# Strip sums of a layer norm: from one TensorE matmul to sixteen small VectorE moves

## The chip, the cores and the metric

The kernel runs on one core of a Trainium2 chip. A core has five engines that run their own instruction queues side by side: TensorE (PE in the profile; its weight loads are listed as PEld), VectorE (DVE), ScalarE (ACT), GpSimd (POOL) and SyncE (SP), which here issues the DMA transfers. They wait for each other by semaphores. The metric is the device time of one execution in microseconds (us). Three runs of the kernel before took 3235.81, 3236.75 and 3239.74 us: median 3236.75 us.

## The reference, cut to what matters

64 graphs of 256 nodes with 512 features each go through three attention steps. `x` is (64, 256, 512), `adj` is (64, 256, 256), all in fp32.

```
# layer 0, 8 heads of 64
Q, K, V = x @ W_q + b_q, x @ W_k + b_k, x @ W_v + b_v
scores  = Q K^T / 8 + (x @ w_g[:D])[:, :, None] + (x @ w_g[D:])[:, None, :] + b_g + log(adj + 1e-9)
y       = softmax(scores) V + x
# layer 1, first half: 8 heads, second half: 1 head of 512
def attention(h, heads, W, a_src, a_dst):
    n = (h - mean(h)) * rsqrt(var(h) + 1e-6) * g + b          # over the 512 features
    v = n @ W;  s = v . a_src;  t = v . a_dst                 # per head
    e = leaky_relu(s[i] + t[j], 0.2) + adj[i, j]
    return softmax(e over j) v + h
z   = attention(y, 8, W1, ...)
out = attention(z, 1, W2, ...)
```

What the change touches is `rsqrt(var(h) + 1e-6)`, the row factor of every node in both norms ("y norm" and "z norm" below), and how the factor of the rows `s` reaches all partitions in the last step.

## The kernel before, in words

**Layout.** Activations are kept transposed: `xT`, `yT` and `zT` are [128 partitions, 4, 256], features across partitions and nodes along the free dimension. The features are permuted so that a block of 32 x 32 stands in each strip of 32 partitions, which is what VectorE's transposition works on.

**The work of one graph** is a generator, `graph(b)` (L477). Every `yield` ends a step; the steps have names in the lists below. In order: `load` (DMA of X and adj), `turn` (X and adj transposed on VectorE, sums for the Winograd products on GpSimd, xT written to DRAM), `V`, `V7`, `V4`, `Q`, `Q7`, `Q4`, `K`, `K7`, `K4` (products of 2 x 2 blocks in seven multiplications instead of eight, `winograd`, L310: five products, then the seventh, then the fourth), two `scores` (matmul and exp), two `mask` (times adj, sum over j), `sums 0` (L378: column sums on TensorE, reciprocal on VectorE, through DRAM to all partitions; x fetched back), `product 0` (L414: attention times V on TensorE), `gather 0` (scaled and added to x on VectorE, which gives yT; begins `rstd_of`), `tokens 1` (ends `rstd_of`), `V1`, `V1 7`, `V1 4` (products with W1, scaled by the row factor as they leave PSUM), `rows 1` (row factors of the 8 heads through DRAM to all partitions), eight steps `weights` (Relu and Exp on ScalarE, adding adj on VectorE), `sums 1`, `product 1`, `gather 1` (gives zT, begins `rstd_of` again and writes Z + bias to DRAM), `tokens 2` (ends `rstd_of`, fetches the rows X2), `V2`, `V2 7`, `V2 4`, `rows 2`, `weights 2`, and two `product 2` (L748 on: TensorE product, reciprocal `rinv`, ScalarE scales, GpSimd adds, SyncE writes the rows out).

**Order.** TensorE's order is written out by hand: `start`, then `period` repeated (an entry is the age of a graph and a step, so six graphs are in flight at once), then `finish`. `tc.manual_schedule` holds TensorE to it. The other engines get their order from the framework's scheduler, which places what is ready as it goes; their queues are then fixed too and run strictly in order. PSUM is a ring of eight banks (`ps`, L159), given out in TensorE's order; a bank is free when its reader is done. The small scaled copies that wait for a partner product (`m1`, `m5`, `u2`) share a ring of four buffers (tag `kept`).

**The norm statistics** (`rstd_of`, L255). `Z` is the strip-wise transposition of yT or zT: [128, 8, 128], where partition 32a + r of block `b` holds a quarter `a` of the features of node 32b + r. `bn_stats` on each of the 8 blocks (L263) gives count, mean and squared deviations of even and odd elements: 6 numbers, so `parts` is [128, 8, 2, 3]. The four quarters of one node lie in four strips of 32 partitions. To add them, before squares the means into the count's place (L265), multiplies by `same` on TensorE (L268; four copies of the 32 x 32 identity in every strip: every partition gets the sum over the four strips), picks its own blocks with `own` (L273), adds up (L278), and forms the variance as mean of squares less square of mean in L282 to L290. `skew` (L289) keeps the worst ratio of squared mean to variance, since this form loses digits where it is large. GpSimd raises to the power -0.5 (L292).

**Row factors** (`target_rows`, L440). For the single head, exp(-0.8 s) of 256 nodes has to stand on all partitions. Usually it goes through DRAM: VectorE transposes (L460), four small transfers write it (L463), one reads it back to all partitions (L473). For the last graph alone (L442) VectorE spreads it to a tile `wide` and TensorE multiplies by the identity (L447 to L450), which leaves the rows in PSUM.

**Guards.** At the end, `note_odd` (L369) tests collected values against bounds, and a slow path recomputes all graphs if any is out of bounds. Collected are `seen` (sums from ScalarE), `extremes` (the running maximum and minimum of all `rinv`, two VectorE operations a graph, L768) and `skew`. `note_odd` of `seen` stands beside the last graph's `rows 2` (L901); that of `extremes` and `skew` is the last work before the final transposition (L906 to L911).

Of the kernel before, what the change touches and what calls it, by code (L numbers as in the profile page):

```python
# [9 lines left out]
F32 = mybir.dt.float32  # L10
# [4 lines left out]
P = 128  # L15
# [5 lines left out]
def kernel(  # L21
# [49 lines left out]
    extremes = const.tile([P, 2, NT], F32, name="extremes")  # L71
    nc.gpsimd.memset(extremes, 1.0)
# [10 lines left out]
    same = const.tile([P, 4, 32], F32, name="same")  # L83
    own = const.tile([P, 4], F32, name="own")
    nc.gpsimd.memset(own, 0.0)
    for a in range(4):
        strip = slice(32 * a, 32 * a + 32)
        nc.gpsimd.tensor_copy(
            same[strip], ident[strip, strip].unsqueeze(1).to_broadcast([32, 4, 32])
        )  # L90
        nc.gpsimd.memset(own[strip, a : a + 1], 0.125)
    skew = const.tile([P, NT], F32, name="skew")
    nc.gpsimd.memset(skew, LOW)

# [57 lines left out]
    with ExitStack() as main:  # L152
# [102 lines left out]
        def rstd_of(xT):  # L255
# [6 lines left out]
            for block in range(2 * KC):  # L262
                nc.vector.bn_stats(parts[:, block].rearrange("p h c -> p (h c)"), Z[:, block, :])  # L263
            mean = parts[:, :, :, 1]
            nc.vector.tensor_tensor(parts[:, :, :, 0], mean, mean, ALU.mult)  # L265
            yield Z
            pt = ps("st")[:, : 12 * KC]
            nc.tensor.matmul(  # L268
                pt, same.rearrange("p c r -> p (c r)"), parts.rearrange("p b h c -> p (b h c)"),
                start=True, stop=True,  # L270
            )
            picked = small.tile([P, NT, 4, 6], F32, name="picked", tag="picked")
            nc.vector.tensor_tensor(  # L273
                picked, pt.rearrange("p (t g i) -> p t g i", t=NT, g=4),
                own.unsqueeze(1).unsqueeze(3).to_broadcast([P, NT, 4, 6]), ALU.mult,
            )
            means = small.tile([P, NT, 3], F32, name="means", tag="means")
            nc.vector.tensor_reduce(  # L278
                means, picked.rearrange("p t g (h c) -> p t c g h", c=3), AX.XY, ALU.add
            )  # L280
            square = small.tile([P, NT], F32, name="square", tag="square")
            nc.vector.tensor_tensor(square, means[:, :, 1], means[:, :, 1], ALU.mult)  # L282
            var = small.tile([P, NT], F32, name="var", tag="var")
            nc.vector.tensor_tensor(var, means[:, :, 0], square, ALU.subtract)
            nc.vector.scalar_tensor_tensor(
                var, means[:, :, 2], 1.0 / 64.0, var, ALU.mult, ALU.add
            )
            nc.vector.scalar_tensor_tensor(square, var, -16.0, square, ALU.mult, ALU.add)
            nc.vector.tensor_tensor(skew, skew, square, ALU.max)  # L289
            nc.vector.tensor_scalar(var, var, 1e-6, None, ALU.add)  # L290
# [78 lines left out]
        def note_odd(v, low, high):  # L369

            bad = work.tile([P, HD + H], F32, name="bad", tag="kept", bufs=4)[:, : v.shape[1]]
            worst = small.tile([P, 1], F32, name="worst", tag="worst")
            for bound, op in ((low, ALU.max), (high, ALU.min)):
                nc.vector.scalar_tensor_tensor(bad, v, bound, v, op, ALU.not_equal)
                nc.vector.tensor_reduce(worst, bad, AX.X, ALU.max)
                nc.vector.tensor_tensor(odd, odd, worst, ALU.max)
# [63 lines left out]
        def target_rows(st, heads, b):  # L440

            if heads == 1 and b == B - 1:  # L442
# [34 lines left out]
        def graph(b):  # L477
# [270 lines left out]
            rinv = small.tile([P, NT], F32, name="rinv2", tag="rinv2")  # L748
            for t in range(NT):
# [16 lines left out]
                if t == NT - 1:  # L766
                    for i, op in enumerate((ALU.max, ALU.min)):
                        nc.vector.tensor_tensor(extremes[:, i], extremes[:, i], rinv, op)  # L768
# [356 lines left out]
```

## Time and profile before

| what | value |
| --- | --- |
| profiled execution, its own time | 3234.22 us |
| its span, first to last instruction | 3232.4 us |
| median of the three runs | 3236.75 us |
| busy: TensorE / VectorE / ScalarE / GpSimd | 97% / 84% / 68% / 33% |
| one graph in the steady part (L268 at 1545.39 and at 1594.12) | 48.7 us |
| TensorE's strip matmul, L268 | 256 instructions, 41.5 us |
| VectorE's L265, the first small operation behind bn_stats | 128 instructions, 154.9 us |

How to read it: times in a timeline are microseconds from the start of the span, first the start, then how long. Small VectorE operations overlap: the next one starts before the former has ended, so the distance from start to start says what one costs in a queue, and the mean duration does not. `out<-in` gives the tiles by name. `[0.54 <-ACT m L525]` is idle time in front of an instruction and what ended it. A TensorE group of the timeline, say `x8`, covers the whole product.

The profiled execution lies 2.5 us (0.1%) under the median of the runs.

### The profile page before, as it was taken

How to read it: one execution, taken by the hardware profiler on the slowest of the kernel's cores; microseconds unless marked ns; L12 is line 12 of the kernel's file. 1: busy time of each engine (PE TensorE's matmuls, PEld its weight loads, DVE VectorE, ACT ScalarE, POOL GpSimd, SP SyncE). 2: the span in 40 equal slices, each digit the busy share in tenths (PEclk: the TensorE clock that was granted, in tenths of full speed). 3: DMA queues.
4: the chain of work that ended last, by engine and by line, in shares of the span. 5: the costliest groups of instructions: out<-in, count | busy, mean ns of one | idle time of the engine just before them, and what ended most of it. 6: DMA issues, size and time to landing. Idle time of an engine off the chain costs nothing. (4 is left out here: it accounts for less than half of the span.)

```text
span 3232.4 us, 77827 instructions
## 1 busy us (share of the span) xinstructions
PE 3135.6 (97%) x28232; PEld 2621.6 (81%) x28232; DVE 2717.1 (84%) x6093; ACT 2188.5 (68%) x5959; POOL 1068.4 (33%) x1315
## 2 busy tenths in 40 slices
PE   7899999999999999999999999999999999999986
PEld 5678888888888888888888888888888888888864
DVE  5788888888888888888888888888888888888885
ACT  3467677677677677676676676676676676676673
POOL 3232332332332332333333333333323423423333
PEclk9999999999999999999999999999999999999998
DMA  4234444444444444444444444444444434444432
GB/s 133 92 118 131 124 131 131 126 127 133 127 128 133 127 124 135 128 122 134 129 122 136 125 126 124 131 130 125 132 124 132 132 123 133 131 123 133 125 116 90
DMA packets 354664, 407.94 MB, mean 126 GB/s; under 512 B 117840, under 2 KB 262496, under 8 KB 354272
## 3 DMA queue, kind: packets, MB, share of 16 engines
q1 hardware_dynamic: 353120, 401.83, 41.6%
q8 instruction: 224, 3.67, 0.5%
q14 instruction: 168, 1.38, 0.1%
q10 hardware_dynamic: 1152, 1.06, 0.1%
HBM read 266.83 MB, written 135.87 MB: 125 GB/s over the span
## 5 line engine op out<-in xcount | busy, mean ns | idle before, releaser
L682 DVE TENSOR_TENSOR ET<-ET,AT 128x512 f32<-128x512 f32 x512 | 363.4, 711 | 239.3 <-ACT ET L676 238.7
L686 ACT ACTIVATE ET<-ET,ends 128x256 f32<-128x256 f32 x1024 | 482.1, 503 | 104.7 <-DVE ET L682 103.6
L676 ACT ACTIVATE ET<-R,f 128x256 f32<-128x256 f32 x1024 | 461.3, 501 | 74.9 <-PE ps_num L425 55.7
L425 PE MATMUL ps_num<-ET,V 128*32 128x256 f32 x8192 | 466.7, 379 | 0.0
L302 POOL TENSOR_TENSOR S<-yT 128x256 f32<-128x256 f32 x64 | 47.7, 746 | 1210.5 <-ACT zT L409 967.6
L765 POOL TENSOR_TENSOR X<-X,weighted 128x256 f32<-128x256 f32 x256 | 210.9, 834 | 545.0 <-ACT weighted L764 536.9
L425 PEld LDWEIGHTS ps_num<-ET,V 128*32 128x32 f32 x8192 | 263.9, 110 | 155.2 <-issue 1.1
L613 DVE TENSOR_TENSOR ET<-ET,AT 128x1024 f32<-128x1024 f32 x256 | 306.6, 1231 | 39.4 <-ACT ET L599 39.4
L599 ACT ACTIVATE ET<-ps_sc,V 128x512 f32<-128x512 f32 x512 | 302.3, 697 | 7.8 <-PE ps_sc L592 7.8
L756 PE MATMUL ps_av<-V,ET 128*128 128x258 f32 (+1 forms) x1024 | 250.7, 389 | 24.3 <-DVE ET L744 24.3
L326 PE MATMUL ps_a<-w,S 128*128 128x264 f32 (+1 forms) x1024 | 268.5, 385 | 4.9 <-ACT m L639 2.9
L326 PE MATMUL ps_b<-w,S 128*128 128x264 f32 (+1 forms) x1024 | 266.6, 383 | 0.8 <-DVE w L131 0.7
L592 PE MATMUL ps_sc<-QT,KT 64*128 64x256 f32 x2048 | 239.4, 383 | 0.0
L263 DVE BATCH_NORM_STATS2 parts<-Z 128x6 f32<-128x128 f32 x1024 | 238.3, 275 | 0.1
L756 PEld LDWEIGHTS ps_av<-V,ET 128*128 128x128 f32 x1024 | 189.8, 196 | 48.9 <-issue 13.0
L326 PEld LDWEIGHTS ps_a<-w,S 128*128 128x128 f32 x1024 | 185.9, 189 | 46.7 <-ACT m L639 6.9
L326 PEld LDWEIGHTS ps_b<-w,S 128*128 128x128 f32 x1024 | 193.8, 189 | 32.5 <-PE ps_a L326 1.1
L592 PEld LDWEIGHTS ps_sc<-QT,KT 64*128 64x128 f32 x2048 | 192.4, 187 | 24.8 <-issue 1.5
L646 ACT ACTIVATE V<-ps_a,rstd 128x257 f32<-128x257 f32 (+1 forms) x128 | 60.0, 469 | 199.2 <-PE ps_a L326 199.2
L434 DVE TENSOR_TENSOR ps_num<-ps_num,R 128x512 f32<-128x512 f32 x256 | 169.9, 687 | 9.6 <-DMA R<-kept 7.0
L702 POOL TENSOR_TENSOR Z<-Z,bw 128x1024 f32<-128x1024 f32 x64 | 175.7, 2745 | 4.1 <-DVE parts L263 3.0
L409 ACT ACTIVATE yT<-yT,columns 128x256 f32<-128x256 f32 x256 | 120.8, 499 | 65.4 <-DMA yT<-kept 65.4
(175 smaller groups left out, 7396.3 us busy)
## 6 DMA issues: line engine op xcount, KB each, us to landing
R<-kept SPq DMA_DIRECT2D x128, 512.0 KB
X<-in_x_dram SPq DMA_DIRECT2D x256, 128.0 KB
kept<-xT SPq DMA_DIRECT2D x64, 512.0 KB
yT<-kept SPq DMA_DIRECT2D x64, 512.0 KB
R<-kept SPq DMA_DIRECT2D x512, 64.0 KB
kept<-yT SPq DMA_DIRECT2D x64, 512.0 KB
kept<-Z SPq DMA_DIRECT2D x64, 512.0 KB
X<-kept SPq DMA_DIRECT2D x512, 64.0 KB
```

Source lines behind the costliest of these rows:

```text
L263: nc.vector.bn_stats(parts[:, block].rearrange("p h c -> p (h c)"), Z[:, block, :])
L326: nc.tensor.matmul(to, A[:, kk, :], B[:, kk, :], start=(first and kk == 0), stop=(kk == 1), skip_group_check=not first,)
L425: nc.tensor.matmul(num[32 * a : 32 * a + 32, m * N : (m + 1) * N], V[:, j, a // 2, a % 2 * P + q * DH + 32 * m :][:, :32], pair[a // 2][:, ...
L592: nc.tensor.matmul(banks[h % 2][:, o : o + N], KT[lo : lo + DH, (q + h) // 2, j * P : (j + 1) * P], QT[lo : lo + DH, (q + h) // 2, :], sta ...
L599: nc.scalar.activation(ET[:, j, i::2, :], banks[i].rearrange("p (h n) -> p h n", n=N), AF.Exp, bias=c[:, j, :],)
L613: nc.vector.tensor_tensor(ET[:, j, :, :], ET[:, j, :, :], AT[:, j, :].unsqueeze(1).to_broadcast([P, 4, N]), ALU.mult,)
L676: nc.scalar.activation(ET[:, j, h, :], R[q][:, h, :], AF.Relu, bias=f[:, j, at : at + 1])
L682: nc.vector.tensor_tensor(two, two, AT[:, j, :].unsqueeze(1).to_broadcast([P, 2, N]), ALU.add)
L686: nc.scalar.activation(ET[:, j, i, :], ET[:, j, i, :], AF.Exp, bias=targets[:, j, 4 * q + i : 4 * q + i + 1],)
L702: nc.gpsimd.tensor_tensor(Z, Z, folded["2"].row.unsqueeze(1).to_broadcast([P, 2 * KC, P]), ALU.add)
L756: nc.tensor.matmul(av[:, :width], ET[:, j, t * P : (t + 1) * P], V2[:, j, n, :width], start=(j == 0), stop=(j == NT - 1),)
L765: nc.gpsimd.tensor_tensor(o[:, cols], o[:, cols], weighted, ALU.add)
```

## The change

Four edits, and new lists.

1. `rstd_of`: the matmul with `same`, the product with `own` and the small operations behind it go. In their place 16 VectorE copies bring, for every pair of strips, the 32 partitions x 2 x 6 numbers of strip `a`'s blocks `g` and `g + 4` to strip `g` of a tile `gathered`, and two `bn_aggr` combine four quarters each to mean and variance. One addition of 1e-6 remains. `same`, `own` and `skew` go.
2. `target_rows`: the way through TensorE is taken for the last three graphs instead of the last one.
3. `rinvs` keeps the inverse sums of all graphs (two columns a graph) in one tile, which replaces `extremes` and its two operations a graph. Those up to graph 55 are tested beside the last graph's `rows 2`, the other 16 columns at the end.
4. `note_odd`: one clamp by both bounds, one comparison, one reduction, one maximum: four operations in a row instead of two chains of three.
5. `start`, `period` and `finish` are new. In a period V1 and its seventh product now come ahead of V, and "V1 4" behind "V7"; `load` moves to the front.

```diff
-            mean = parts[:, :, :, 1]
-            nc.vector.tensor_tensor(parts[:, :, :, 0], mean, mean, ALU.mult)
+            gathered = small.tile([P, NT, 4, 6], F32, name="gathered", tag="gathered")
+            for a in range(4):
+                for g in range(4):
+                    nc.vector.tensor_copy(
+                        gathered[32 * g : 32 * g + 32, :, a, :],
+                        parts[32 * a : 32 * a + 32, g::4].rearrange("p t h c -> p t (h c)"),
+                    )
             yield Z
-            pt = ps("st")[:, : 12 * KC]
-            nc.tensor.matmul(
-                pt, same.rearrange("p c r -> p (c r)"), parts.rearrange("p b h c -> p (b h c)"),
-                start=True, stop=True,
-            )
-            picked = small.tile([P, NT, 4, 6], F32, name="picked", tag="picked")
...
-            nc.vector.tensor_tensor(skew, skew, square, ALU.max)
-            nc.vector.tensor_scalar(var, var, 1e-6, None, ALU.add)
+            moments = small.tile([P, NT, 2], F32, name="moments", tag="moments")
+            for t in range(NT):
+                nc.vector.bn_aggr(moments[:, t, :], gathered[:, t].rearrange("p a c -> p (a c)"))
+            var = small.tile([P, NT], F32, name="var", tag="var")
+            nc.vector.tensor_scalar(var, moments[:, :, 1], 1e-6, None, ALU.add)
...
-            for bound, op in ((low, ALU.max), (high, ALU.min)):
-                nc.vector.scalar_tensor_tensor(bad, v, bound, v, op, ALU.not_equal)
-                nc.vector.tensor_reduce(worst, bad, AX.X, ALU.max)
-                nc.vector.tensor_tensor(odd, odd, worst, ALU.max)
+            nc.vector.tensor_scalar(bad, v, low, high, ALU.max, ALU.min)
+            nc.vector.tensor_tensor(bad, bad, v, ALU.not_equal)
+            nc.vector.tensor_reduce(worst, bad, AX.X, ALU.max)
+            nc.vector.tensor_tensor(odd, odd, worst, ALU.max)
...
-            if heads == 1 and b == B - 1:
+            if heads == 1 and b >= B - 3:
...
-            rinv = small.tile([P, NT], F32, name="rinv2", tag="rinv2")
+            rinv = rinvs[:, NT * b : NT * b + NT]
...
-                if t == NT - 1:
-                    for i, op in enumerate((ALU.max, ALU.min)):
-                        nc.vector.tensor_tensor(extremes[:, i], extremes[:, i], rinv, op)
...
         period = [
-            (3, "V1 4"), (5, "tokens 2"), (2, "scores"), (2, "scores"), (1, "V4"),
-            (3, "rows 1"), (2, "mask"), (5, "V2"), (3, "weights"), (2, "mask"),
-            (5, "V2 7"), (2, "sums 0"), (2, "product 0"), (5, "V2 4"), (1, "Q"),
-            (5, "rows 2"), (1, "Q7"), (4, "sums 1"), (2, "gather 0"), (3, "weights"),
-            (3, "weights"), (3, "weights"), (5, "weights 2"), (4, "product 1"),
-            (0, "turn"), (1, "Q4"), (1, "K"), (1, "K7"), (3, "weights"),
-            (5, "product 2"), (1, "K4"), (5, "product 2"), (3, "weights"),
-            (2, "tokens 1"), (0, "V"), (2, "V1"), (3, "weights"), (4, "gather 1"),
-            (2, "V1 7"), (0, "V7"), (-1, "load"), (3, "weights"),
+            (4, "weights"), (3, "V1 7"), (1, "V"), (1, "V7"), (5, "tokens 2"),
+            (3, "V1 4"), (3, "rows 1"), (2, "scores"), (2, "scores"), (2, "mask"),
+            (-1, "load"), (2, "mask"), (1, "V4"), (3, "weights"), (5, "V2"),
+            (5, "V2 7"), (2, "sums 0"), (2, "product 0"), (5, "V2 4"), (5, "rows 2"),
+            (1, "Q"), (1, "Q7"), (4, "sums 1"), (3, "weights"), (3, "weights"),
+            (2, "gather 0"), (5, "weights 2"), (0, "turn"), (3, "weights"),
+            (3, "weights"), (4, "product 1"), (2, "tokens 1"), (1, "Q4"), (1, "K"),
+            (1, "K7"), (5, "product 2"), (4, "gather 1"), (1, "K4"), (5, "product 2"),
+            (3, "weights"), (3, "weights"), (2, "V1"),
         ]
...
+                    note_odd(rinvs[:, : NT * (B - 8)], 1e-25, 1e25)
                     note_odd(seen[:, : 4 * B], -1.0, 1e25)
                     note_odd(seen[:, 4 * B :], -1.0, 3600.0)
...
-        note_odd(extremes.rearrange("p i t -> p (i t)"), 1e-25, 1e25)
-        note_odd(skew, LOW, 0.0)
+        note_odd(rinvs[:, NT * (B - 8) :], 1e-25, 1e25)
```

## The prediction

> **What bounds the kernel now.** I read the share of busy time first, then busy time by stretch, then TensorE's waits in the steady part, then the rows of the instructions that the change touches, and last one period in order of time.
>
> ```profile
> PE 3135.6 (97%) x28232; PEld 2621.6 (81%) x28232; DVE 2717.1 (84%) x6093; ACT 2188.5 (68%) x5959; POOL 1068.4 (33%) x1315
> ```
> ```profile
> 300.00:2800.00 2500.00, 2484.74 (x22678) 2089.66 (x22680) 2146.21 (x4814) 1750.62 (x4784) 833.65 (x1023) 1.00 0.43 129
> ```
> ```profile
> PE ps_a L333 <- ACT m L525: 14.7, 25, 1.7
> ```
>
> The second line has the columns stretch, length, then busy time of PE, PEld, DVE, ACT and POOL, and the granted clock. From 300 to 2800 us TensorE is busy 99.4% at full clock, and its only listed wait there (to 2900 us) is 14.7 us, on ScalarE's copies in the K product. One graph takes 48.7 us there (the strip sums' matmul of the z norm stands at 1545.39 and again at 1594.12 us), so this wait is 0.28 us a graph. VectorE has 14% idle. So TensorE's work sets the time, as long as the others keep their appointments inside the period; the question is whether they still do.
>
> ```profile
> L268 PE MATMUL ps_st<-parts,same 128*128 128x48 f32 x256 | 41.5, 244 | 6.4 <-DVE parts L265 6.3
> ```
> ```profile
> L265 DVE TENSOR_TENSOR parts<-parts 128x16 f32<-128x16 f32 x128 | 154.9, 1210 | 0.1
> L666 DVE TENSOR_SCALAR f<-ends 128x16 f32<-128x16 f32 x64 | 10.7, 167 | 0.0
> L768 DVE TENSOR_TENSOR extremes<-extremes,rinv 128x2 f32<-128x2 f32 x128 | 41.3, 361 | 0.0
> ```
> ```profile
> 1531.29 1.19 DVE L258 STREAM_TRANSPOSE Z<-yT 128x1024 f32<-128x1024 f32 x1
> 1532.40 0.92 DVE L682 TENSOR_TENSOR ET<-ET,AT 128x512 f32<-128x512 f32 x1
> 1533.24 1.63 DVE L263 BATCH_NORM_STATS2 parts<-Z 128x6 f32<-128x128 f32 x8
> 1534.80 0.67 DVE L682 TENSOR_TENSOR ET<-ET,AT 128x512 f32<-128x512 f32 x1
> 1535.39 0.17 DVE L265 TENSOR_TENSOR parts<-parts 128x16 f32<-128x16 f32 x1
> 1535.58 0.88 DVE L744 SCALAR_TENSOR_TENSOR ET<-R,f,AT 128x256 f32<-128x256 f32 x2
> ```
> ```profile
> 1537.93 0.38 ACT L525 COPY m<-ps_b 128x256 f32<-128x256 f32 x1
> 1538.19 0.52 ACT L686 ACTIVATE ET<-ET,ends 128x256 f32<-128x256 f32 x1
> 1538.61 0.72 ACT L517 ACTIVATE AT<-AT,eps 128x512 f32<-128x512 f32 x1
> 1539.22 0.51 ACT L686 ACTIVATE ET<-ET,ends 128x256 f32<-128x256 f32 x1
> 1539.62 0.36 ACT L525 COPY u<-ps_a 128x256 f32<-128x256 f32 x1
> ```
> ```profile
> 1540.03 1.16 PE L333 MATMUL ps_a<-S,wk 128*128 128x128 f32 x8
> ```
>
> The last three fences are one stretch on three engines. VectorE runs it without a gap; ScalarE's copy u, in order behind exponentials and AT+eps that need VectorE, ends just as TensorE starts the seventh K product, which needs it. That appointment has no slack.
>
> **What goes, per graph (two norms).** On TensorE the strip matmul: its two instructions push the next one back 0.25 us in the y norm (1508.10 to 1508.35) and 0.16 in the z norm (1545.39 to 1545.55): 0.40 us. On VectorE, by the distance from start to start: L265 2.4 us (0.17 in the y norm; 2.38 at 1501.98, where it stands until GpSimd's 2.77 us Z<-Z,bw L702, begun at 1501.55, ends), the small operations L273 to L289 2.2, the two extremes 0.6: 5.2 us.
>
> **What comes, per graph.** 32 copies of 32 partitions x 12 elements, 4 bn_aggr, one of the old small operations kept per norm. No row of before is a VectorE operation that reads one group of 32 partitions and writes another. Bounds: two small operations that don't depend on each other follow at 0.08 us (L458 at 1509.58, L666 at 1509.66); two that do, at 0.20 (L288 at 1510.12, L289 at 1510.32). So 16 cost 1.3 to 3.2 us. I take 0.167, the whole duration of L666, the nearest in size and kind (one input, SBUF to SBUF), without overlap: 2.7 us a norm. I lean away from the 0.08 since each copy changes the output's partitions, which no overlapped pair of before does. bn_aggr has no row; 0.07 to 0.2 by the same rows, 0.3 a pair. Sum per graph 5.4 + 0.6 + 0.2 = 6.2 us against 5.2: VectorE stays at about 88% of a period and doesn't become the bound by its sum.
>
> [...]
>
> **Where it falls.** In the new program the 16 copies stand in one block straight behind the eight bn_stats; the old chain let L682 and others in between. Behind the y block now come the pair L744 and the next L682, and on ScalarE the exponentials of that L682, AT+eps and copy u stand in this order. Replayed with the rows: bn_stats done 1534.85; copies to 1537.55; L744 pair 0.8; L682 0.6, 1538.95; exponential pair 0.85, 1539.8; AT+eps 0.6; u 0.3, 1540.7. K's seventh product starts 1540.75. Without any stall it would start at 1534.70 + 5 x 0.895 = 1539.18: stall 1.57, of which the old lists paid 0.28 on average. The cover is 2.0 us: up to 0.125 a copy, L682 is done before ScalarE asks.
>
> VectorE's queue goes on: AT transposes 0.7, bn_aggr 0.3, L682 0.6, L691 1.1, three KT puts 1.0, L434 and L438 twice each 2.4, rinv 0.1, L682 0.6, xT 1.2: rinv of the second strip at about 1547.1. Then L682 (behind GpSimd, 0.3) 1547.9, Z 1549.05, L682 1550.0, on ScalarE two exponentials and u of V1, 1551.3. TensorE is at V1's seventh product at 1540.75 + 0.9 + 1.75 + 0.9 + 1.75 + 5 x 0.89 = 1550.5: another stall of 0.9. The new lists put V1 ahead of V and "V1 4" behind V7, so xT and the puts of V1 have 1 to 5 us of cover; this hides the z block (copies end 1554.3, the put of c that frees the buffer for V's m5 at 1554.8, product 3 of V due 1555.8).
>
> Waits added and steps moved: bn_aggr waits for the copies, with a put of V (y: L682, L691) queued behind it on VectorE, and GpSimd's rstd behind that; both norms' rstd are due more than 5 us later (V1's first scaled copy after 1546.9, V2 after "V4"), so nothing; if that cover went, 0.6 us a graph. SyncE issues ten transfers less (rows of two graphs). The step "load" moves to the front of the period with its eight issues (X 2.4 us of SP, A 1.8), but X still stands ahead of the fetch of X2 and of kept<-rows, as at 1504.74 to 1511.67, and SP has idle stretches behind (1516.1 to 1520.4): nothing; at most 2.4 us of delay to R, which ScalarE takes up some 3 us after it has landed.
>
> Per graph: +1.57 - 0.28 + 0.9 - 0.40 = +1.8 us. 58 graphs run in the steady part (about 250 to 3100 us): +104 us. The other six save the matmul alone: -2.4.
>
> **Start and end.** Fewer GpSimd constants (4 copies of 0.29 us and some memsets) lie beside the first loads: nothing; if they were not covered, -1.9. The row factor of graphs 61 and 62 on TensorE replaces rows through DRAM: TensorE's waits of 12.6 us (3166 to 3179) and 5.2 us (3197.4 to 3202.6) before ps_av. The first is the time of the last graph's own weights, which stays on the chain; of the second the last graph's rstd comes earlier by at most 3.1 us (3209.9 now; 3206.8 by bn_stats from 3201.1, copies, aggr, pow), -3.1. The end: 3.1 us from the last rinv (3222.14) to the last odd (3225.2) become four dependent operations of 0.2 or so: -2.1. note_odd of the early inverse sums is 4 operations beside the last graph. One-off costs of the new start and finish lists are not readable from rows: -5 to +10, taken as 0.
>
> The sum is made against the profiled execution, 3234.2 us (span 3232.4 and 1.8 around it), 2.5 under the median of the runs, within 0.1%. 3234.2 + 104 - 2.4 - 5.2 = 3330.6: forecast 3330, its own range 3270 to 3380 (each stall off by half).
>
> **Rivals.**
> *The cover holds: faster.* Copies follow at 0.08: the block is 1.3 us, K's seventh product stays where it is, V1's stall shrinks to 0 to 0.15. Then -0.40 or -0.25 a graph: 58 of these, -2.4, -5.2 give 3203 to 3212. For it: VectorE's sum hardly grows, the new lists give V1 slack. It decides below 2.0 us a block (0.125 a copy), where the two stalls together just eat the matmul's 0.40.
>
> *Copies collide with GpSimd.* L702 starts as the last bn_stats of the z norm ends, that is under the copies. If a copy must stand aside as L265 does, the z block ends 2.8 us later, V's m5 buffer comes free at 1557.6, ScalarE copies until 1557.95, product 3 of V is 2.2 us late: +128 us, 3458; with GpSimd waiting instead, the put of V1 waits behind L691 and half of it is lost, 3394. For it: the 2.38 us row. Against it: one-input operations run beside GpSimd freely in before (bn_stats), and only two-input rows are stretched. [...]
>
> *The change does little:* stalls of 0.4 take the 0.4 saved, end gains aside: 3230 to 3240.
>
> **How the numbers follow.** Forecast 0.40, collision 0.28, cover holds 0.28, little 0.04. A change of under 0.2% (6.5 us) can't be told from none. Faster: cover holds, less a bit: 0.27. Same 0.04, slower 0.69. The range must reach the fast case (3203) and into the collision case; 3200 to 3440 leaves out half of the collision's full price and the far ends, about 2 in 10.
>
> **What would show it.** Copy rows by start to start: 0.08, 0.17, or some of 2.8 us under L702's successor. TensorE waits on ScalarE's copies in K (u) and in V1 (u), 1 to 1.6 us each, once per graph; period of the scores 50.5 us against 48.7. L268 gone. ps_av waits at the end shorter. I am wrong if the copies overlap, if ScalarE's order has more slack than this one period shows (it is a period with a stall of 0.54; others have less), or if the start and finish lists cost tens of us.

## The result, and the profile after

The kernel after takes 3689.96 us (median of four runs, 3684.24 to 3692.77) against 3236.49 us: a ratio of 1.140, 95% interval 1.138 to 1.142. The prediction was 3330 us with a range of 3200 to 3440. The profiled execution took 3684.24 us, with a span of 3682.4.

The share of busy time, and the stretch from 300 to 2800 us (columns as in the prediction):

```profile
PE 3265.2 (89%) x27984; PEld 2660.5 (72%) x27984; DVE 3005.0 (82%) x7237; ACT 2205.9 (60%) x5959; POOL 1092.9 (30%) x1304
```
```profile
300.00:2800.00 2500.00, 2256.93 (x19517) 1847.14 (x19516) 2069.40 (x4986) 1533.08 (x4153) 742.87 (x890) 0.96 0.36 112
```

TensorE, busy 99.4% of this stretch before, is busy 90%, at a granted clock of 0.96 instead of 1.00. VectorE is not full either: 83%. A graph takes 55.98 us instead of 48.72 (distance of the bn_stats of the y norm over 46 graphs). The difference of 7.26 us, times the 58 graphs of the steady part, is 421 of the 453 us lost; the rest lies in fill and end.

TensorE's waits between 300 and 3300 us (total, times, longest). In a Winograd product ScalarE makes copies of single products, `m` and `u`; a "put" below is the VectorE operation that adds such a copy to another product and writes a finished block.

```profile
PE ps_b L299 <- ACT m L498: 187.3, 54, 3.5
PE ps_a L306 <- ACT u L498: 79.5, 53, 1.9
PE ps_a L299 <- ACT u L612: 19.1, 52, 0.5
```

The second is the wait in K that the prediction replayed: 1.50 us a graph. The third is V1's: 0.37. The first, the largest, it had not: 3.47 us a graph in V, before the fifth product in the order of issue ("product 3 of V" in the prediction). (L299 and L306 were L326 and L333; L498, L612 and L621 were L525, L639 and L648.) The rows of the moves on the page:

```profile
L254 DVE COPY gathered<-parts 32x12 f32<-32x12 f32 x2048 | 586.9, 287 | 25.6
L261 DVE BATCH_NORM_AGGREGATE moments<-gathered 128x2 f32<-128x24 f32 x256 | 46.2, 221 | 0.0
```

The mean of 287 ns hides two kinds. In the y norm sixteen copies take 2.82 us, in the z norm 6.84. VectorE's y block of one period, then its z block in order of time, the whole block first, then five of its copies one by one, then the put that follows:

```profile
1735.77 2.82 DVE L254 COPY gathered<-parts 32x12 f32<-32x12 f32 x16
...
1752.43 6.84 DVE L254 COPY gathered<-parts 32x12 f32<-32x12 f32 x16
...
1752.77 2.23 DVE L254 COPY gathered<-parts 32x12 f32<-32x12 f32 x1
1755.01 0.66 DVE L254 COPY gathered<-parts 32x12 f32<-32x12 f32 x1
1755.69 0.67 DVE L254 COPY gathered<-parts 32x12 f32<-32x12 f32 x1
1756.37 0.67 DVE L254 COPY gathered<-parts 32x12 f32<-32x12 f32 x1
...
1757.23 0.61 DVE L254 COPY gathered<-parts 32x12 f32<-32x12 f32 x1
...
1759.31 0.49 DVE L621 SCALAR_TENSOR_TENSOR V<-ps_c,rstd,m 128x264 f32<-128x264 f32 x1
```

GpSimd in the same time:

```profile
1752.59 2.38 POOL L675 TENSOR_TENSOR Z<-Z,bw 128x1024 f32<-128x1024 f32 x1 [0.36 <-DVE parts L250]
1754.93 0.72 POOL L275 TENSOR_TENSOR S<-zT 128x256 f32<-128x256 f32 x1
1755.61 0.72 POOL L278 TENSOR_TENSOR S<-zT 128x256 f32<-128x256 f32 x1
1756.30 0.72 POOL L276 TENSOR_TENSOR S<-S,zT 128x256 f32<-128x256 f32 x1
1757.09 0.72 POOL L277 TENSOR_TENSOR S<-zT,S 128x256 f32<-128x256 f32 x1
```

Each of the five long copies ends as one of these five operations ends (1752.77 + 2.23 = 1755.00 beside 1752.59 + 2.38 = 1754.97, and so on), and GpSimd's next operation starts before the copy that follows (1754.93 beside 1755.01, the others 0.07 to 0.14 us ahead). The same holds in all 53 z blocks between 300 and 3300 us: five copies over 0.25 us in each, and each of these 265 ends 0.02 to 0.04 us behind the end of one of the five operations. The eleven others take 0.14 to 0.17 us. Then ScalarE and TensorE:

```profile
1759.89 0.38 ACT L498 COPY m<-ps_b 128x257 f32<-128x257 f32 x1 [5.08 <-DVE V L621]
```
```profile
1755.91 1.03 PE L299 MATMUL ps_a<-wv,S 128*128 128x257 f32 x4
1760.41 1.84 PE L299 MATMUL ps_b<-wv,S 128*128 128x257 f32 x4 [3.47 <-ACT m L498]
1762.05 1.92 PE L299 MATMUL ps_a<-wv,S 128*128 128x257 f32 x4
```

The put of c (L621) stands behind the copies, it frees the buffer for ScalarE's m, and TensorE's next product needs the bank that m reads. Behind the wait two products take 1.84 and 1.92 us instead of 1.03: the granted clock is 0.50 from 1760.63 to 1764.04 (lines in the last section). Of the 50 waits of this kind between 300 and 3100 us, 48 were followed by such a stretch. From the start of the product that waited to the end of the next scores product it took 8.5 us on average over all 50, and 6.5 behind the two that were not: 2.0 us a graph.

Together V's wait 3.47, the clock behind it 2.0, K's wait 1.50 less the 0.28 of before, V1's 0.37, less the 0.40 of the strip matmul make 6.7 of the 7.26 us; what the rest consists of is not shown.

### The profile page after: what moved, and what is told of

Its sections match the earlier page's. It is cut to its first block, busy times and chain, and to the rows that moved or that the text cites. A ratio compares the mean times of both kernels' runs of the same rounds, so it can differ in the third digit from the quotient of the medians.

```text
span 3682.4 us, 78506 instructions
## 1 busy us (share of the span) xinstructions
PE 3265.2 (89%) x27984; PEld 2660.5 (72%) x27984; DVE 3005.0 (82%) x7237; ACT 2205.9 (60%) x5959; POOL 1092.9 (30%) x1304
## 5 line engine op out<-in xcount | busy, mean ns | idle before, releaser
L254 DVE COPY gathered<-parts 32x12 f32<-32x12 f32 x2048 | 586.9, 287 | 25.6
L655 DVE TENSOR_TENSOR ET<-ET,AT 128x512 f32<-128x512 f32 x512 | 388.3, 760 | 238.3 <-ACT ET L649 238.2
L299 PE MATMUL ps_b<-wv,S 128*128 128x257 f32 x512 | 181.9, 490 | 210.7 <-ACT m L498 207.8
L265 POOL TENSOR_TENSOR rstd<-var,mhalf 128x2 f32<-128x2 f32 x128 | 96.4, 753 | 789.2 <-DVE var L263 784.5
L299 PE MATMUL ps_a<-w,S 128*128 128x264 f32 (+1 forms) x1024 | 277.4, 394 | 36.5 <-ACT u L612 21.7
L299 PEld LDWEIGHTS ps_b<-wv,S 128*128 128x128 f32 x512 | 113.8, 234 | 251.4 <-issue 234.2
L738 POOL TENSOR_TENSOR X<-X,weighted 128x256 f32<-128x256 f32 x256 | 233.0, 930 | 146.4 <-ACT weighted L737 146.4
L299 PE MATMUL ps_b<-w,S 128*128 128x264 f32 (+1 forms) x1024 | 269.8, 386 | 0.5 <-ACT m L612 0.5
L299 PEld LDWEIGHTS ps_a<-w,S 128*128 128x128 f32 x1024 | 185.1, 191 | 97.2 <-ACT u L612 56.7
L565 PE MATMUL ps_sc<-QT,KT 64*128 64x256 f32 x2048 | 247.1, 391 | 0.0
L498 ACT COPY m<-ps_b 128x257 f32<-128x257 f32 (+1 forms) x128 | 47.2, 369 | 308.3 <-DVE V L621 299.9
L306 PE MATMUL ps_a<-S,wk 128*128 128x128 f32 x1024 | 144.4, 284 | 95.9 <-ACT u L498 89.0
```

The costliest lines, as they stand in the source:

```text
L254: nc.vector.tensor_copy(gathered[32 * g : 32 * g + 32, :, a, :], parts[32 * a : 32 * a + 32, g::4].rearrange("p t h c -> p t (h c)"),)
L299: nc.tensor.matmul(to, A[:, kk, :], B[:, kk, :], start=(first and kk == 0), stop=(kk == 1), skip_group_check=not first,)
L306: nc.tensor.matmul(to[:, m * P : (m + 1) * P], B[:, kk, m * P : (m + 1) * P], A[:, kk, :], start=(first and m == kk == 0), stop=(kk == 1), ...
L565: nc.tensor.matmul(banks[h % 2][:, o : o + N], KT[lo : lo + DH, (q + h) // 2, j * P : (j + 1) * P], QT[lo : lo + DH, (q + h) // 2, :], sta ...
L655: nc.vector.tensor_tensor(two, two, AT[:, j, :].unsqueeze(1).to_broadcast([P, 2, N]), ALU.add)
L738: nc.gpsimd.tensor_tensor(o[:, cols], o[:, cols], weighted, ALU.add)
```

## The experiments

Theories: **A**, the z block, torn by GpSimd, makes most of the loss; **B**, the new lists do; **C**, the number of moves alone, as forecast. All ratios are to runs of the kernel before on the same chip (medians 3236 to 3241 us); times without an interval are single runs. "us a graph" is the distance of bn_stats over 46 graphs.

| run | us | ratio, 95% interval | us a graph |
| --- | --- | --- | --- |
| after | 3690 | 1.140 (1.138 to 1.142) | 55.98 |
| y_moves_only | 3338 | 1.031 (1.029 to 1.032) | 50.31 |
| z_moves_only | 3530 | 1.089 (1.087 to 1.091) | 53.43 |
| moves_by_reduce | 3438 | 1.062 (1.060 to 1.064) | 52.06 |
| no_z_addition | 3433 | | 51.85 |
| reduce_by_target | 3438 | 1.061 (1.059 to 1.062) | 52.07 |
| copies_by_target | 3691 | | 55.98 |
| moves_in_strip | 3443 | | 52.02 |
| reduce_in_strip | 3318 | 1.025 (1.023 to 1.026) | 50.11 |
| five_kept | 3618 | 1.118 (1.116 to 1.119) | 54.69 |
| lists_on_before | 3439 | 1.061 (1.060 to 1.063) | 51.82 |
| moves_old_lists | 3677 | 1.135 (1.133 to 1.137) | 55.54 |
| reduce_by_target_old_lists | 3470 | 1.070 (1.069 to 1.072) | 52.31 |
| no_moves | 3327 | 1.026 (1.025 to 1.028) | 50.49 |
| no_moves_old_lists | 3231 | 0.998 (0.997 to 0.999) | 48.55 |
| tail_alone | 3245 | 1.001 (1.000 to 1.002) | 48.79 |
| moves_by_dma | 3814 | 1.178 (1.177 to 1.180) | 58.05 |

### Which of the two blocks

`rstd_of` gets a flag: copies in the y norm alone in one kernel, in the z norm alone in the other; the norm without them takes its blocks from `parts`.

```diff
-        def rstd_of(xT):
+        def rstd_of(xT, move):
...
-                nc.vector.bn_aggr(moments[:, t, :], gathered[:, t].rearrange("p a c -> p (a c)"))
+                take = gathered[:, t].rearrange("p a c -> p (a c)") if move else parts[:, 4 * t : 4 * t + 4].rearrange("p b h c -> p (b h c)")
+                nc.vector.bn_aggr(moments[:, t, :], take)
```

> The kernel after with the sixteen copies in the y norm alone; in the z norm bn_aggr reads four blocks of one strip from parts, so the z statistics are those of other numbers. The prediction put the whole loss into this block (stalls of 1.57 in K and 0.9 in V1): by it 3330. Theory A (the torn z block makes 5.3 of the 7.3 us a graph): K's and V1's waits stay as in the kernel after, 1.5 and 0.4 us, V's goes: 50 to 51 us a graph, 3310 to 3370.

> The counterpart: copies in the z norm alone, the y statistics are those of other numbers. By the prediction the z block is hidden: 3205, or 3327 as without any moves. Theory A: torn by GpSimd to 5 to 7 us, V's third product waits 2.5 to 3.5 us for ScalarE's copy m and runs slowly behind it: 53 to 56 us a graph, 3500 to 3680.

TensorE's waits, first with the moves in y alone:

```profile
PE ps_a L308 <- ACT u L500: 86.3, 58, 1.9
PE ps_a L301 <- ACT u L614: 19.4, 53, 0.5
```

With the moves in z alone:

```profile
PE ps_a L301 <- DVE V L623: 149.7, 56, 3.5
PE ps_a L308 <- ACT m L500: 81.2, 56, 2.6
```

With the y block alone the time is 3338 us, near the 3330 that the prediction had for the whole change, with K's wait at 1.49 us (forecast 1.57) and V1's at 0.37 (0.9). The z block, forecast as hidden, makes a wait of 2.7 us a graph, here for VectorE's put of V itself; K's wait is for the copy m here, not for u. A graph takes 55.98 us with both blocks and 50.31 with the y block alone, so the z block costs 5.67 us, which fits the 3.47 of V's wait and the 2.0 of the clock. With both blocks copied the time is 352 us above that of the y block alone. C as the whole story falls.

### What makes the z block long

```diff
-                    nc.vector.tensor_copy(
+                    nc.vector.tensor_reduce(
                         gathered[32 * g : 32 * g + 32, :, a, :],
-                        parts[32 * a : 32 * a + 32, g::4].rearrange("p t h c -> p t (h c)"),
+                        parts[32 * a : 32 * a + 32, g::4].rearrange("p t h c -> p t (h c)").unsqueeze(3),
+                        AX.X, ALU.max,
```

> The kernel after, each of the sixteen copies written as a tensor_reduce with maximum over an axis of one element: the same numbers move between the same strips, by another VectorE operation. If only the copy has to take turns with GpSimd (theory A with a mode that belongs to the copy), no move is stretched beyond 0.3 us, the z block takes as long as the y block (2.8 to 3.5 us), the wait for the scaled copy in V goes, and the time is 3290 to 3400 us. If any small VectorE operation gives way to GpSimd, the z block stays near 6.8 us and the time near 3690. Theory B: 3690. Theory C: 3690 is not explained by it at all, and nothing changes here.

The moves of one stretch (shortest, median and longest in ns) and TensorE's waits:

```profile
L254 DVE TENSOR_REDUCE gathered<-parts x615: 135/157/163, 1000.0 to 1989.8; 32x12 f32<-32x12 f32 x154
```
```profile
PE ps_a L307 <- ACT u L499: 79.4, 57, 1.8
PE ps_a L300 <- ACT m L499: 63.1, 56, 1.2
PE ps_a L300 <- ACT m L613: 51.3, 56, 0.9
```

No move is stretched, though 304 of the 614 that start in this stretch run beside an operation of GpSimd; both blocks take 2.69 us, the clock stays at 1.00 between 300 and 2800 us, and 252 us are gone. So of copy and reduction only the copy is stretched beside GpSimd (up to 2.23 us in the block above; none of these reductions took more than 0.163). The time ends above the 3290 to 3400 expected: three waits of 1.4, 1.1 and 0.9 us remain. ScalarE's work stands in another order here than in the kernel after (in V1 the wait is for m, not for u), so these waits are not those of the kernel after one by one.

```diff
-            nc.gpsimd.tensor_tensor(
-                Z, Z, folded["2"].row.unsqueeze(1).to_broadcast([P, 2 * KC, P]), ALU.add
-            )
```

> The kernel after without GpSimd's addition of the bias to Z, which stands beside the z block's third copy (this addition is left out; the bias is zero in these inputs). Theory A: the copy that took 2.23 us takes 0.17, the four others beside the S operations stay at 0.6 to 0.7 each: z block 4.8 us, V's wait 1.2 to 1.6 instead of 3.5, hardly a slow product behind it: 51.5 to 53 us a graph, 3420 to 3510. If the block's length has another cause, 6.8 and 3690.

```profile
L254 DVE COPY gathered<-parts x624: 144/166/676, 1000.4 to 1988.8; 32x12 f32<-32x12 f32 x156
```
```profile
PE ps_a L306 <- ACT u L498: 89.3, 58, 1.8
PE ps_b L299 <- ACT m L498: 78.2, 56, 1.4
```

The copy of 2.23 us is gone, those of 0.6 to 0.68 stay, the z block is 4.77 us, V's wait 1.40, and no wait is followed by slow products: the clock is 1.00 from 300 to 2800 us. As A expected: one operation of GpSimd, 2.1 us of stretch, is worth some 257 us.

### What one move costs

Three kernels change the strips between which a move goes or their order: `gathered[32 * a ...]` written from `parts[32 * a ...]` (in strip), and the two loops exchanged (by target).

> The kernel after, with every copy writing to the strip that it reads (the same sixteen operations of 32 x 12 numbers, but the four quarters of a node are not brought together, so the statistics are those of other numbers: this part of the computation is changed). Tells what changing strips costs. If a copy is held until the last has ended because its output begins in another strip, the y block of 2.82 us falls to 1.3 to 1.7 us (0.08 to 0.1 a copy, three of four in the same strip as their predecessor). Otherwise it stays at 2.8. The z block: under theory A it still meets GpSimd, 4 to 6 us, with fewer interruptions since it is shorter; time 3450 to 3650. Under theory C it follows the y block, about 3250.

> The kernel after with the moves as tensor_reduce over an axis of one, and the two loops exchanged, so that four moves in a row write the same strip. The result of the computation is that of the kernel after. If a move is held only where the strip it writes changes, 12 of 16 cost 0.075 and 4 cost 0.17: a block is 1.6 us (1.3 to 1.8); if the strip it reads counts too, it stays at 2.7. At 1.6 us the block is inside the cover of 2.0 us that the prediction read for K's seventh product, nothing collides with GpSimd, and by theory C the time is 3200 to 3240; by theory B it stays above 3300.

> The kernel after with the two loops of the copies exchanged: four in a row write the same strip, and read four different ones. Copies inside one strip took 0.075 us, copies that change both strips 0.176; as tensor_reduce, four writes to one strip from four strips took 0.169. If the strip that is written decides, the y block is 1.6 us here (and it was the reduction that is slow by itself); if the strip that is read, or a difference between the two, decides, it stays at 2.8. The z block is torn as in the kernel after, less often if it is shorter; time 3440 to 3450 (short) or 3690 (long).

> The kernel after with the moves as tensor_reduce that write the strip they read (statistics of other numbers: the quarters are not brought together). Not torn by GpSimd, and short if what holds a move is the change of strips: 1.3 to 1.7 us a block (at 0.169 each it would stay 2.7 and 3438). The prediction's rival said that below 2.0 us a block nothing stalls: 3203 to 3212. A straight line through the runs (K's wait 1.4 at 2.69 us, 0.4 at 1.59 with copies in strip) leaves 0.3 to 0.4 us in K and nothing elsewhere: 3230 to 3280.

Moves, from start to start: in strip 0.075 us as a copy and 0.072 as a reduction, where the strip is that of the move before, and 0.17 and 0.16 where it changes; a block takes 1.59 and 1.52 us. With the strip written kept for four moves and the strip read changing, 0.178 and 0.169: the blocks stay at 2.82 and 2.69, and the times do not change. In the kernel after, where the strip read is kept for four moves and the strip written changes, a copy costs 0.176. So it was enough here that one of the two strips changed. As sixteen moves for all pairs of strips never repeat both, no order of theirs should be shorter; that is an estimate from these numbers. The y block in strip as copies, and the reductions by target:

```profile
1621.57 1.59 DVE L254 COPY gathered<-parts 32x12 f32<-32x12 f32 x16
```
```profile
1625.46 2.70 DVE L254 TENSOR_REDUCE gathered<-parts 32x12 f32<-32x12 f32 x16
```

The in-strip copies are torn all the same: their z block is 5.67 us, V's wait 2.30:

```profile
PE ps_b L299 <- ACT m L498: 128.7, 56, 2.3
```

TensorE's waits with reductions in strip:

```profile
PE ps_a L300 <- ACT m L613: 59.5, 59, 5.8
PE ps_a L307 <- ACT u L499: 20.8, 58, 0.6
PE ps_a L300 <- ACT m L499: 19.8, 56, 0.8
```

Beside moves_by_reduce this is the same order of work with blocks of 1.52 instead of 2.69 us: K's wait falls from 1.39 to 0.36, V's from 1.13 to 0.35, V1's stays at about 0.9. K's wait falls by 0.88 per us of block and would, as an estimate from these two runs, be gone at 1.1 us, not at the 2.0 of the prediction; neither the 3203 to 3212 of its rival nor the 3230 to 3280 expected before this run was reached at 1.52 us (3318).

### The ring of scaled copies

```diff
-                k = work.tile([P, HD + H], F32, name=name, tag="kept", bufs=4)[:, :width]
+                k = work.tile([P, HD + H], F32, name=name, tag="kept", bufs=5)[:, :width]
```

> The kernel after with five buffers instead of four in the ring of scaled copies (tag kept); to make room, parts and gathered have one buffer each, and the inverse sums are not collected and not checked at the end (that guard is left out). The copies stay torn. If V's third product waits for that ring alone (the put of c of V1 frees the buffer of m5, theory A), the buffer that the put frees is now needed one copy later, by u2 two products on: the wait falls from 3.5 to some 1.6 us, and the slow products behind it with it: 3500 to 3580. If it waits for something else as well, it stays at 3.5 and 3690.

```profile
PE ps_a L298 <- ACT u L497: 138.0, 55, 2.5
PE ps_a L305 <- ACT u L497: 82.5, 55, 1.9
```

The wait for m is gone and comes back one copy later, for u, as expected; at 2.5 us it fell by 1.0, not by 1.9, and the slow products stayed (behind all 52 such waits between 300 and 3100 us). The buffer was the link, but one more (with one buffer less for `parts` and `gathered`, as said above) gains 72 us, not 110 to 190. Why u waits 0.9 us longer than the sum said is not shown.

### The lists

> The kernel before with edits 2, 4 and 5 (row factors of three graphs on TensorE, the shorter note_odd, all new lists); the strip matmul, its small operations, extremes and skew stay, so VectorE gets no moves. Theory A (the copies behind the z norm's bn_stats are torn apart by GpSimd's five operations, 6.85 us a block, and hold up V's third product): without copies nothing is left of the loss; steady period 48.3 to 48.8 us, 3215 to 3240 us in all. Theory B (the new lists put V1 and V where their inputs come late, whatever gives the statistics): over 3500. Theory C (the number of moves alone, as forecast, two stalls of 1.57 and 0.9 us): also no loss here, 3215 to 3240.

```profile
PE ps_st L268 <- DVE parts L265: 124.2, 56, 3.4
```

This run was meant to part A from B and does not: 3439 us lies far above what A and C expected (3215 to 3240) and below what B did (over 3500). In the new lists "tokens 1" stands only one TensorE step ("product 1") behind "gather 0", so the strip matmul of the y norm is issued before the work that feeds it is done, and TensorE waits 2.2 us for it. The new lists can't carry the old strip sums; the kernel after has no such matmul. So the old lists were given the moves, and both lists no moves at all:

```diff
-                nc.vector.bn_aggr(moments[:, t, :], gathered[:, t].rearrange("p a c -> p (a c)"))
+                nc.vector.bn_aggr(moments[:, t, :], parts[:, 4 * t : 4 * t + 4].rearrange("p b h c -> p (b h c)"))
```

> The kernel before with edit 1 alone (16 copies and bn_aggr in place of the strip matmul and its small operations); old lists, extremes stay, skew and its check go. Theory A: the z norm's copies still meet GpSimd's Z addition and S operations, since these wait for the same bn_stats and zT; some copies last 0.6 to 2.3 us, TensorE waits behind a kept buffer or a product just after; 3400 us or more. Theory B: nothing but the copies' 1 us a graph more on VectorE, 3240 to 3300. Theory C: K's stall of 1.3 us more a graph and V1's, 3330 or a little more, since the old lists give V1 less room.

> The kernel before with edit 1 alone, the moves as tensor_reduce in the order of the strip they write; old lists. Tells, beside the same moves in the new lists, what the lists are worth once a block is 1.6 us. Theory C: the old lists pay K's stall of 0.3 us at most, less 0.40 for the strip matmul: 3210 to 3250. Theory B: faster here than in the new lists by 50 us or more.

> The kernel after without the sixteen moves: bn_aggr reads four blocks of one strip from parts directly, so the statistics are those of other numbers (the bringing together of the four quarters of a node is left out). Everything else, the new lists too, stays. If the moves are all that costs time (theory A for the torn block, theory C for the rest), no product waits for ScalarE's copies, a period is 48.3 us and the time 3195 to 3215 us. If part of the 200 us that stay when the moves are made by tensor_reduce belongs to the new lists (theory B), it stays here: 3250 to 3440.

> The kernel before with edit 1 but without the sixteen moves: bn_aggr reads four blocks of one strip from parts, so the statistics are those of other numbers (the four quarters of a node are not brought together). Old lists, so the partner of the new lists without moves (3327 us, a wait of 1.1 to 2.5 us a graph for ScalarE's copy m in K). If that wait belongs to the new lists (theory B), the old ones have none: 48.3 us a graph, 3205 to 3225. If it comes of the order in which ScalarE and VectorE take their work once the strip matmul is gone, whatever the lists, there is a wait of about 1 us a graph here too: 3260 to 3330.

| moves | old lists | new lists |
| --- | --- | --- |
| none | 3231 | 3327 |
| sixteen reductions a norm | 3470 | 3438 |
| sixteen copies a norm | 3677 | 3690 |

Without moves, TensorE's waits in the new lists, and then in the old:

```profile
PE ps_a L299 <- ACT m L491: 86.0, 56, 2.5
```
```profile
PE ps_a L300 <- ACT m L492: 10.8, 23, 1.8
```

By the ratios, which compare runs of one chip, copies cost 210 (old lists) and 252 us (new) more than reductions (A), and reductions 234 and 116 us more than nothing. The new lists cost some 90 us without moves and gain 31 with reductions. In their run without moves ScalarE's copy m in K stands behind AT+eps and the exponentials around it, an order that the scheduler chose; it stands in z_moves_only too, so it comes with the y block left out. In the kernel after and in y_moves_only m comes ahead of AT+eps and u behind. So K's wait has no single owner, and how much of the 90 us is the lists and how much that order stays open. Of the four runs, moves_old_lists came out as A had it and no_moves in the range of B. The other two missed: reductions on the old lists were expected at 3210 to 3250 us (C) or 50 us faster than on the new (B), and are 32 us slower; no moves on the old lists were expected at 3205 to 3225 or 3260 to 3330.

The first row tells what there was to gain: on the old lists even a kernel without any moves gains only 0.2%. Without the 0.40 us of the matmul and the small operations behind it a graph takes 48.55 us instead of 48.72.

### The end, and another way to move

tail_alone is the kernel before with `if heads == 1 and b >= B - 3:` and the new `note_odd`.

> The kernel before with edit 2 and the shorter note_odd alone; old lists, strip matmul, extremes and skew stay. The steady part does not change (48.7 us a graph). By the prediction's working the row factor through TensorE gains up to 3.1 us in the last three graphs and the shorter chain of the last test 1 to 2 us: 3230 to 3237, ratio 0.997 to 1.000. All three theories expect the same.

TensorE near the end, in order of time:

```profile
3179.64 0.66 PE L268 MATMUL ps_st<-parts,same 128*128 128x48 f32 x2 [3.88 <-DVE parts L265]
...
3198.28 1.92 PE L384 MATMUL ps_su<-R,ones 128*32 128x128 f32 x28 [5.92 <-DVE R L691]
...
3216.65 0.66 PE L268 MATMUL ps_st<-parts,same 128*128 128x48 f32 x2 [3.54 <-DVE parts L265]
```

The waits of 12.6 and 5.2 us for the rows are gone, and TensorE waits for the strip sums and for the last graph's weights instead. Nothing of the 4 to 5 us expected is gained: the run is 4 us slower (1 to 7), at the edge of what can be told.

moves_by_dma writes `parts` to DRAM with one transfer of SyncE and reads it back with four, on the old lists:

```diff
+            mixed = dram.tile([P, 2 * KC, 6], F32, name="mixed", tag="mixed")
+            nc.sync.dma_start(out=mixed, in_=parts.rearrange("p b h c -> p b (h c)"))
+            for g in range(4):
+                nc.sync.dma_start(
+                    out=gathered[32 * g : 32 * g + 32],
+                    in_=mixed.rearrange("(a r) (t g) i -> g r t a i", a=4, g=4)[g],
+                )
```

> The kernel before with edit 1, the moves made by SyncE's transfers: one writes parts to DRAM, four read it back, each to one strip of gathered; old lists, extremes stay. VectorE gets neither copies nor the old small operations (5 us a graph less), TensorE no strip matmul (0.40 us a graph less). The factor is due more than 5 us after bn_stats; two transfers one behind the other take some 4 to 5. If that holds and the transfers hold up no others: 3205 to 3225. If V1's first scaled copy comes late by 1 to 2 us a graph, or the queue's other transfers do: 3260 to 3360. It has the order of ScalarE's work that follows from the missing matmul, so if that order alone makes a wait (as in the run without moves on the old lists), 3260 to 3330 too.

SyncE's issues, VectorE, GpSimd and ScalarE after a bn_stats that ends at 1509.55:

```profile
1509.58 0.34 SPq L254 DMA_DIRECT2D mixed<-parts  x1
...
1514.02 2.60 SPq L256 DMA_DIRECT2D gathered<-mixed  x4
```
```profile
1522.56 0.37 DVE L263 BATCH_NORM_AGGREGATE moments<-gathered 128x2 f32<-128x24 f32 x2
```
```profile
1524.95 1.60 POOL L267 TENSOR_TENSOR rstd<-var,mhalf 128x2 f32<-128x2 f32 x1
```
```profile
1526.59 0.48 ACT L614 ACTIVATE m<-ps_a,rstd 128x264 f32<-128x264 f32 x1 [3.01 <-POOL rstd L267]
```

The reads are issued 4.4 us after the write, behind transfers of adj; bn_aggr runs 13.0 us after bn_stats, behind the next norm's bn_stats in VectorE's queue; the factor comes 3 us late for V1. At 3814 us the run is far outside both ranges expected. The sum of "4 to 5 us" was an estimate that left out both queues.

## Why the prediction was wrong

**The step that failed** is "this hides the z block (copies end 1554.3, the put of c that frees the buffer for V's m5 at 1554.8, product 3 of V due 1555.8)". It gave the z block the y block's 2.7 us, and put what a copy loses beside GpSimd at nothing. The block took 6.84, the put came 4 us later, and product 3 waited 3.47 us: the chain was named right, and the length put into it was wrong. With the clock behind it (2.0 us) that is 5.5 of the 7.26 us a graph. y_moves_only, moves_by_reduce and no_z_addition show it from three sides. Even the cover was right, 0.65 us by the prediction's own times (1555.8 less 1554.8 and 0.35 for the copy): in the three kernels that differ in the block's length and keep ScalarE's order, V's wait is 3.47 at a block of 6.84, 2.30 at 5.67 (moves_in_strip) and 1.40 at 4.77 (no_z_addition), a line that ends at 3.4 us. By it a block of 2.7 would have been hidden in that order; in the other order of the reduction run it was not (a wait of 1.13 at 2.69).

**The collision rival** had the mechanism and 28% of the chance, and its full price of 3458 was 230 us too low. It counted one operation of GpSimd, L702, at 2.8 us. There were five, since the four S operations follow L702 and each falls between two copies. Its argument against, "one-input operations run beside GpSimd freely", rested on bn_stats (0.25 to 0.30 us each in before, beside GpSimd or alone). The copy has one input too and took 0.61 to 2.23 us where it met GpSimd; the reduction, with one input as well, kept 0.16 (at most 0.163 in moves_by_reduce).

**The clock** was in no case of the prediction: 2.0 us a graph behind V's wait.

**The price of a move**: 0.167 us taken, 0.176 measured in the y norm; bn_aggr 0.35 a pair against 0.3. Right, and for the reason given, the change of the output's strip (0.176 where it changes, 0.075 where neither strip does), though the strip read counts as well (0.178 where it alone changes).

**K and V1**: 1.57 and 0.9 forecast, 1.50 and 0.37 measured; y_moves_only gives 3338 against 3330. That the sum of these stalls and this run agree is in good part luck: without any moves the new lists already lose some 85 us against before, in another order of ScalarE's work, so the y block alone adds only 11 us to them. That lists could cost something of their own was left out of the sum.

**The threshold of the fast rival**, 2.0 us a block, contradicts the replay beside it: a stall of 1.57 at a block of 2.7 ends at 1.1, and 1.1 is what the two reduction runs give.

**Start and end**: -5.2 us forecast. tail_alone, which has the new row factor and test but not the lists, gives +4 (1 to 7), so the 5.2 us of gain are shown by no run. In the kernel after, the part outside the steady stretch grows with the period and can't be told apart.

**SyncE's issues and the step load**, costed at nothing: among TensorE's waits after there is none for a transfer, nor for what GpSimd makes. That stands.

## What to carry to other kernels

Price a new operation by its kind: two VectorE operations of one input and one size differed more than tenfold beside GpSimd here (up to 2.23 us against 0.16), and GpSimd got in five times between the sixteen short copies of one block. When a replay names the operation that a block delays, replay it also with the block at its upper bound; here that alone would have shown the 3.5 us. Before taking work away from a bound engine, measure the kernel with that work left out: it gained 0.2%, so on those lists no way of doing it had much more to gain.

## What the hardware showed that was not expected

**A wait of TensorE cost more than its length where it left one window of the clock's grid mostly empty.** The traces record the granted clock. In them it is 1.00 or 0.50, and its steps lie on a grid of 3.41 us. Four windows of that grid in the kernel after, around V's wait (columns as above: the second number is the window's length, the third TensorE's busy time; the third from the end is the granted clock):

```profile
1753.80:1757.22 3.42, 3.14 (x15) 2.41 (x13) 3.36 (x5) 0.38 (x1) 3.34 (x5) 1.00 0.42 157
1757.22:1760.63 3.41, 0.22 (x1) 0.25 (x2) 3.26 (x12) 0.71 (x2) 0.59 (x1) 1.00 0.50 144
1760.63:1764.04 3.41, 3.41 (x9) 2.68 (x9) 2.19 (x8) 0.04 (x1) 0.70 (x1) 0.50 0.33 85
1764.04:1767.46 3.42, 3.42 (x28) 2.77 (x29) 1.15 (x6) 2.21 (x6) 0.00 (x0) 1.00 0.03 8
```

The wait leaves TensorE busy for 0.22 us of the second window, and in the third it is granted half the clock. In the kernel after, 751 windows between 300 and 3100 us are at full clock. Each of the 48 with TensorE busy for less than 41% was followed by one at half clock, of the 674 with 52% or more none was, and of the 29 between one was. Before has 820 windows there, all at full clock, the emptiest busy for 68%. Counted over all 18 traces there are 14325 windows at full clock: each of the 288 under 41% was followed by one at half clock, none of the 13725 with 52% or more, and 72 of the 312 between. As an estimate from these counts (3.41 us less 52%, less 41%), it took some 1.6 to 2.0 us without work inside one window, and a wait shorter than a window was enough, or not, as it lay: 48 of 50 waits of 3.5 us were followed by half clock (kernel after), 52 of 52 of 2.5 us (five_kept, where a graph takes 16.0 windows, so that the wait lies alike each time), 13 of 53 of 2.3 us (moves_in_strip), 26 of 54 of 1.7 to 3.4 us (lists_on_before), none of 161 of 0.6 to 1.8 us (moves_by_reduce), but 24 of 50 of about 1.15 us where a second of 0.85 us followed one product later (moves_old_lists). The mean granted clock from 300 to 2800 us is 0.96, 0.97, 0.99, 0.98, 1.00 and 0.96 in these six.

**GpSimd got in between the copies of a train.** In the kernel after, the first operation of GpSimd (2.38 us) held one copy for 2.23 us until it was over, and each of the four after it held another, for 0.61 to 0.67; GpSimd's four short ones took 0.72 us each. The number of copies that meet one is not fixed: five a z block here, three in z_moves_only (a block of 5.93 us), one in moves_old_lists.
